# The rows of the second norm turned by VectorE and DRAM instead of TensorE, in a transformer block of Strassen products

## The chip, the cores and the metric

One core of one Trainium2 chip. The time is device microseconds of the program on that core, the median of the runs that are named beside it. The profile is that of one execution; its own time is given beside its span.

## The reference

What is computed is one transformer block with conditioning, in float32: 8 sequences of 1024 tokens, width 512, 16 heads of 32, hidden width 2048, all with biases.

```python
mod = silu(condition) @ Wada + bada
sh_a, sc_a, gt_a, sh_m, sc_m, gt_m = split(mod, 6)
xm = layernorm(x, g1, be1) * (1 + sc_a) + sh_a
x = x + gt_a * attention(xm, Wqkv, Wproj, bproj)      # causal, 16 heads
xm = layernorm(x, g2, be2) * (1 + sc_m) + sh_m
x = x + gt_m * (gelu(xm @ W1 + b1) @ W2 + b2)
```

## The kernel before

**Blocks and windows.** The tokens are cut into 16 blocks n of 512, two per sequence; an even n is the first half of a sequence, an odd n the second. All products of rows and weights (q, k, v, the projection, up, down) are of Strassen's kind with seven products of half size instead of eight; a step named T1 to T4 is a sum of quarters of the rows, S1 to S4 one of the weights. The quarters of the rows are B11, B21, B22 and T1 in the tile `xm` (features on partitions, tokens in the row) and T2, T3, T4 in the tile `t`. One product takes two weight pieces (128x512, 256 KB), and each piece is used by 16 matmuls of 32 columns x 256. The seven products of one step go through three PSUM banks; each is evicted by VectorE (L197, a sum with an earlier partial result such as u2 or u4) or ScalarE (L192, a copy), and the next product that needs this bank waits for that.

**The order of the work** is written by a planner in Python, while the program is built. It keeps a modelled clock for each engine (`now`), and the instructions of each engine come in the order in which the planner issues them. Attention of block n (scores L1602, their maxima on VectorE L1619, the second scores L1683 and L1695, the exponential on ScalarE L1708, the weighted sum L1736) is spread over the linear steps of window n, which the table `plan` lists. In window w the block n = w - 1 is projected, normed and taken through up and down, and q, k of block w + 1 and v of block w are made. `fetch` (L336) loads weight pieces nine ahead on SP's queue, each when a piece nine earlier has been used.

**From rows to `xm`.** `normalize` (L617) makes statistics on VectorE and the normed rows on ScalarE (L653). `modulated` (L732) turns them, so that features come to the partitions, and applies the gain and the shift that the conditioning gives. It does so in two ways, and `is_turned` (L377) chooses:

- by TensorE: for each of four chunks of features, four 128x128 transposes into a PSUM bank (L769), then gain and shift on the way out of the bank, by ScalarE (L784) or VectorE (L778). Before the change all blocks of the second norm go this way, and blocks 0 to 3 of the first.
- by VectorE and DRAM (`turn_rows`, L702): four transposes of 32x32 squares on VectorE (L708), four DMAs that put the squares of 32 partitions into a DRAM tile (`put`, L719), one DMA that gets the whole tile back in the turned order (`get`, L725), then gain and shift in place in SBUF (L784, L778). Before the change blocks 4 to 15 of the first norm go this way. The DMAs are kept in the list `transfers` and issued on SP's queue by `run_transfers` (L575), one after the other as the modelled clock passes; the apply is planned for 5000 ns after the get.

Both are followed by T1 (L792) and T2, T3, T4 (L794, and L162 or L165 by VectorE or GpSimd).

**The residual** rows (`xr`) of a block are loaded by four DMAs in `load_xr`, get the projection and the down products added on VectorE and GpSimd (L162, L165), and are stored by `store` (L1189) in four DMAs, two after each half. Those are on SP's queue too, in which every DMA waits for its own inputs, with all that stand behind it.

Of the kernel before, what the change touches and what calls it, by code (L numbers as in the profile page):

```python
# [22 lines left out]
def kernel(  # L23
# [176 lines left out]

    def matmul(ps, lhsT, rhs, start, stop, reads=(), bank=None):

        for j in range(HPG):
            r = slice(j * hd, (j + 1) * hd)
            nc.tensor.matmul(  # L205
                ps[r, :], lhsT[:, r], rhs, start=start, stop=stop, skip_group_check=True
            )
# [30 lines left out]
        0: [("load_xa", 2), ("preps",), ("k", 1), ("norm_a", 2), ("gates", "a"), ("q", 1)]  # L238
        + [("mod", 4), ("at", 2), ("v", 1), ("mod", 3), ("gates", "m")],
    }  # L240
    late = []
    for w in range(1, NB):
        n = w - 1
        m = mlp_steps(n)
        even = blocks[n][1] == 0
        rows_a = [("rows", blocks[n][0], "a")] if even else []
        rows_m = [("rows", blocks[n][0], "m")] if even else []
        own = m[:1] + ([("load_xa", w + 2)] if w + 2 < NB else []) + m[1:3]
        own += [("norm_a", w + 2)] if w + 2 < NB else []
        if w == NB - 1:  # L250
            steps = late[:1] + [("load_xr", n)] + rows_a + [("proj", n), ("mt", n)] + late[1:]
            steps += [("v", w)] + rows_m + own + m[3:6]
            late = m[6:]
        else:

            steps = late + [("v", w), ("load_xr", n)] + rows_a + [("proj", n), ("k", w + 1)]
            if w == 1:
                steps = [("load_xr", n)] + rows_a + [("k", w + 1), ("proj", n)]
            steps += [("mt", n), ("q", w + 1)] + rows_m + own
            at = [("at", w + 2)] if w + 2 < NB else []  # L260
            if blocks[w][1] == 0:

                late = m[3:4] + at + m[4:]
            else:
                steps += m[3:4] + at + m[4:6]
                late = m[6:]
        plan[w] = steps
    n = NB - 1
    plan[NB] = [("load_xr", n), late[0], ("beside", ("proj", n)), late[1], ("mt", n)] + mlp_steps(n)

    plain_proj = (NB - 2, NB - 1)
    kept_sums = {}
# [99 lines left out]
    cond_sb = tmp.tile([P, TB], F32, tag="y", name="cond_sb")[:B, :]  # L372
    nc.sync.dma_start(cond_sb, cond)

    SQ = 32
# [326 lines left out]
    def turn_rows(key, tiles, xm):  # L702

        squares = xm.rearrange("p c (j r) -> p (c j) r", r=P)
        there = kept.tile([D, TB], F32, tag=f"turned_{int(key[1:]) % 2}", name=f"turned_{key}")

        def turn(t):
            nc.vector.transpose(  # L708
                squares[:, :, ts(t, SQ)], tiles[t].rearrange("p (k r) -> p k r", r=SQ)
            )  # L710
            note("DVE", 700, [("hat", key, t)], [])
            if t == NTT - 1:
                ready = now["DVE"] + SYNC
                for a in range(P // SQ):
                    transfers.append((ready, lambda a=a: put(a)))
                transfers.append((ready + 5000, get))

        def put(a):
            nc.sync.dma_start(  # L719
                there[:, ts(a, P)].rearrange("(k r) n -> r k n", r=SQ),  # L720
                squares[a * SQ : (a + 1) * SQ, :, :],
            )

        def get():
            nc.sync.dma_start(xm, there.rearrange("(c p) n -> p c n", p=P))  # L725
            written["spread", key] = queue_free[0] + 5000

        written["spread", key] = NEVER
        for t in range(NTT):
            add_job(lambda t=t: turn(t), [("hat", key, t)])  # L730

    def modulated(key, gain, shift, b, guards):  # L732
        for t in ("B11", "B21", "B22", "T1", "T2", "T3", "T4"):
# [77 lines left out]
        return bank  # L811

    qTs, kTs, vs = {}, {}, {}
    projected, valued = set(), set()
    xm_of, hTs, hidden = {}, {}, set()

    SUMS = (("S1", "A21", "A22", ALU.add), ("S2", "S1", "A11", ALU.subtract),
# [78 lines left out]
    def strassen(step, x, dest, target, row, done, put=None, after={}):  # L896
# [14 lines left out]
        def product(a, t, bank=None):  # L911
            start = bank is None
            reads = [(x, t)] + ([("sums", *step, a)] if raw and a[0] == "S" else [])
            for i in range(2):
                for k in range(2):
                    if i + k:
                        yield [], []
                    elif start:
                        yield reads, [BANK]
                        bank = lin_bank()  # L920
                    else:
                        yield reads, [("l", bank)]
# [3 lines left out]
                    lhsT, rhs = (second, first) if row else (first, second)  # L926
                    matmul(
                        banks[bank][:, ts(i, HB)], lhsT[:, ts(i, P)], rhs,
                        start and i + k == 0, k == 1, reads, bank,
                    )  # L930
# [57 lines left out]
        tail_key[0] = key  # L988
        start(tail())

    def project_T(step, store, pool, tag, done):

        n = step[1]
        dst = pool.tile([P, NC, TB], F32, tag=tag, name=f"{tag}_{n}")
# [100 lines left out]
    def project_out(n):  # L1095
# [7 lines left out]
        last = n == NB - 1  # L1103
        begun = []

        def begin(t):

            bank = yield from accumulate(
                [(attT[:, c, ts(t, P)], piece(at[c])) for c in range(NC - 1)], [("att", n)], False
            )  # L1110
            begun.append(bank)

        for t, xt in enumerate(tiles):
            if last:
                while len(begun) <= max(t, 1):
# [1 line left out]
                bank = begun[t]  # L1117
                yield [("att", n, t)], []
                matmul(
                    banks[bank], attT[:, NC - 1, ts(t, P)], piece(at[NC - 1]), False, True,  # L1120
                    [("att", n, t)], bank,
                )
            else:
                bank = yield from accumulate(
                    [(attT[:, c, ts(t, P)], piece(at[c])) for c in range(NC)], [("att", n)]
                )
            y = tmp.tile([P, D], F32, tag="y", name=f"y_{n}_{t}", bufs=2)
            ky = y_key("proj", True)
# [59 lines left out]

    def store(n, t):  # L1189
        b, h = blocks[n]  # L1190
        for i in (2 * t, 2 * t + 1):
            r0 = h * TB + i * P
            nc.sync.dma_start(out[b, r0 : r0 + P, :], residual[n][:, i, :])
        stored[n + 1] = max(stored.get(n + 1, 0.0), due([("xr", n, 2 * t), ("xr", n, 2 * t + 1)]))

    def down(n, part):
# [19 lines left out]
        def product(operand):  # L1216
# [3 lines left out]
            for i in range(NQ):  # L1220
                p = next(at)
                for k in range(2):
                    c = 2 * i + k
                    hT = hTs[n, 2 * kh + c // NC][:, c % NC, tokens]
                    for m in range(2):
# [3 lines left out]
                        else:  # L1229
                            yield [], []  # L1230
                        matmul(
                            banks[bank][:, ts(m, HB)], hT[:, ts(m, P)], halves(p)[:, k, :],
                            c + m == 0, c == 2 * NQ - 1, reads, bank,
                        )
                release(p)
# [94 lines left out]
    def perform(step):  # L1330
# [12 lines left out]
        elif kind == "load_xr":  # L1343
            n = step[1]
            b, h = blocks[n]
            if n == NB - 2:
                xr = kvp.tile([P, NTT, D], F32, tag="kT", name=f"xr_{n}")
            else:
                xr = xrp.tile([P, NTT, D], F32, tag="xr", name=f"xr_{n}")
            residual[n] = xr  # L1350
            for t in range(NTT):
                r0 = h * TB + t * P
                nc.sync.dma_start(xr[:, t, :], x[b, r0 : r0 + P, :])
                landed = max(now["PE"], stored.get(n, 0.0)) + LANDING + 700 * t
                written["xr", n, t] = landed
        elif kind == "norm_a":
            key = f"a{step[1]}"
# [466 lines left out]
    def attend():  # L1824
        previous = None
        for n in range(NB):
# [19 lines left out]
            stream["rate"] = planned_time(n) / mine * (0.7 if n == 0 else 1.0)  # L1846
            written["free for k", n + 2 if n % 2 else n + 1] = 0.0
            written["free for k", n + 1] = 0.0
            for g, k, n_slots, upto in slots:
                if (n, g) == groups[-1]:  # L1850
                    margin[0] = -2000
# [66 lines left out]
    needs = sum(exp_need(parts) for n in range(NB) for g in range(NC) for parts in weight_units(n, g))  # L1918
    needs += sum(score_need(*unit) for unit in units)
    for n in range(NB):  # L1920
        written["attended", n] = NEVER
        written["v done", n] = NEVER
        written["m used", n] = NEVER
# [79 lines left out]
```

## Time and profile before

| | before |
| --- | --- |
| median of 3 runs | 3483.92 us (3483.72 to 3483.95) |
| the profiled execution, its own time | 3487.44 us |
| its span, from the first to the last instruction | 3485.7 us |
| granted TensorE clock | 1.000 |
| TensorE busy in the span | 3448.3 us |

In the page's groups, a row reads: line, engine, operation, output <- inputs by the program's names (numbers left out), shapes, count | busy us, mean ns of one | idle of the engine just before them, and what ended it. A row of the waits reads: engine, tile, line <- what was waited for: us in total, times, longest. A row of a timeline reads: start in us from the span's start, duration, engine, line, operation, tiles, count, and in brackets the idle before it with its releaser. A row of the DMAs reads: tiles, queue, kind, count, size of one, median us from issue to landing. One float32 matmul leaves two records in the trace. PE is TensorE, DVE VectorE, ACT ScalarE, POOL GpSimd, SP SyncE with its DMA queue.

### The profile page before, as it was taken

The page shows a single profiled execution, that of the slowest core. Times are in us where ns is not written, and L with a number is a line of the kernel's source. Part 1 is how long each engine was busy: PE and PEld are TensorE (multiplying, and loading weights), DVE is VectorE, ACT ScalarE, POOL GpSimd, SP SyncE. Part 2 cuts the span into 40 slices and gives each one's busy share as a digit, 9 for nine tenths or more (in the row PEclk, how much of TensorE's full clock was granted, in tenths as well). Part 3 has the DMA queues.
Part 4 walks back from the last instruction along what each step waited for, and adds up shares of the span by engine and source line. Part 5 has one row for each costly group of instructions (what it writes and reads, how often), then busy time and mean ns, then how long its engine had stood idle before and what let it go on. Part 6 is the DMA issues. An engine that isn't in the chain of part 4 may idle for free.

```text
span 3485.7 us, 122756 instructions
## 1 busy us (share of the span) xinstructions
PE 3448.3 (99%) x55618; PEld 1776.1 (51%) x55618; DVE 1905.0 (55%) x2136; ACT 1286.7 (37%) x1420; POOL 2074.5 (60%) x2209
## 2 busy tenths in 40 slices
PE   8999999999999999999999999999999999999999
PEld 5544455445554554545545455454554545545445
DVE  6765664554645556465564655645546455554463
ACT  2335243352433524235152352514524244241531
POOL 3676755675466664576645766557664576644640
PEclk9999999999999999999999999999999999999999
DMA  6843334335353353633536335363443534435334
GB/s 213 271 144 86 117 110 150 120 105 172 107 167 102 105 174 104 186 95 100 173 98 186 98 111 159 101 186 98 129 140 101 183 101 135 130 100 153 90 121 136
DMA packets 350523, 466.84 MB, mean 134 GB/s; under 512 B 27460, under 2 KB 212092, under 8 KB 350004
## 3 DMA queue, kind: packets, MB, share of 16 engines
q1 hardware_dynamic: 349808, 458.73, 43.8%
q8 instruction: 438, 7.18, 0.9%
q14 instruction: 81, 0.66, 0.1%
q10 hardware_dynamic: 196, 0.28, 0.0%
HBM read 416.90 MB, written 41.99 MB: 132 GB/s over the span
## 4 chain that ended last, share of the span: by engine, by line
PE 94%; DVE 3%; POOL 1%; ACT 1%; issue 0%; DMA 0%; SPq 0%; DVEq 0%; ACTq 0%; POOLq 0%
PE bank L205 65%; PE sc L1602 9%; PE po L1736 8%; PE st L1695 7%; PE st L1683 3%; DVE mx L1619 2%; PE bank L1757 2%; PE bank L769 1%; PE bank L1657 1%; POOL pT L1821 0%; DVE sc L1616 0%; POOL mcols L1640 0%; DVE pT L1818 0%; POOL mcols L1641 0%; DMA ada<-in_L_cond_Wada_dram 0%
## 5 line engine op out<-in xcount | busy, mean ns | idle before, releaser
L1821 POOL TENSOR_TENSOR pT<-pT,pT 128x256 f32<-128x256 f32 (+3 forms) x1254 | 1174.5, 972 | 210.3 <-ACT pT L1708 119.2
L1708 ACT ACTIVATE pT<-st 128x2048 f32<-128x2048 f32 x288 | 541.1, 1879 | 1001.1 <-PE st L1695 908.8
L205 PE MATMUL bank<-w,hT 128*32 128x256 f32 x14336 | 795.5, 379 | 0.0
L1619 DVE TENSOR_REDUCE mx<-sc 128x4 f32<-128x2048 f32 (+3 forms) x384 | 665.6, 1754 | 140.3 <-PE sc L1602 133.7
L205 PEld LDWEIGHTS bank<-w,hT 128*32 128x32 f32 x14336 | 448.8, 110 | 335.6 <-issue 29.2
L205 PE MATMUL bank<-xm_m,w 128*32 128x256 f32 x8192 | 498.8, 380 | 0.0
L205 PE MATMUL bank<-t_m,w 128*32 128x256 f32 x6144 | 384.2, 380 | 0.1
L205 PEld LDWEIGHTS bank<-xm_m,w 128*32 128x32 f32 x8192 | 253.6, 110 | 238.8 <-issue 76.0
L1713 POOL TENSOR_SCALAR_AFFINE_SELECT pT<-pT 128x512 f32<-128x512 f32 x256 | 164.8, 661 | 308.8 <-ACT pT L1708 306.9
L1602 PE MATMUL sc<-kT,qT 32*128 32x512 f32 (+3 forms) x3072 | 329.1, 520 | 2.9 <-DVE mx L1619 1.9
L1616 DVE TENSOR_TENSOR sc<-sc,mask 128x1024 f32<-128x1024 f32 (+1 forms) x160 | 162.9, 1018 | 276.2 <-PE sc L1602 217.6
L1736 PE MATMUL po<-pT,v 128*32 128x512 f32 (+3 forms) x3072 | 306.0, 493 | 0.0
L1695 PE MATMUL st<-qT,kT 32*128 32x512 f32 (+3 forms) x3072 | 299.8, 486 | 0.0
L205 PEld LDWEIGHTS bank<-t_m,w 128*32 128x32 f32 x6144 | 193.0, 110 | 180.8 <-issue 54.2
L205 PE MATMUL bank<-xm_a,w 128*32 128x256 f32 x3968 | 248.8, 381 | 1.3 <-ACT xm_a L784 1.1
L197 DVE TENSOR_TENSOR hT<-bank,u_u 128x512 f32<-128x512 f32 x192 | 129.1, 686 | 151.2 <-PE bank L205 149.0
L165 POOL TENSOR_TENSOR qT<-top,rec 128x512 f32<-128x512 f32 x60 | 77.1, 1285 | 219.8 <-ACT rec L1775 219.8
L1602 PEld LDWEIGHTS sc<-kT,qT 32*128 32x128 f32 x3072 | 129.4, 183 | 150.9 <-ACT pT L1708 61.8
L205 PE MATMUL bank<-w,qT 128*32 128x256 f32 (+1 forms) x2944 | 191.4, 399 | 1.3 <-DVE qT L1782 1.3
L1153 ACT ACTIVATE hT<-hT,cols 128x512 f32<-128x512 f32 x256 | 164.2, 711 | 55.0 <-DVE hT L197 54.4
L205 PE MATMUL bank<-t_a,w 128*32 128x256 f32 x2944 | 183.3, 380 | 0.0
L165 POOL TENSOR_TENSOR hT<-hT,hT 128x1024 f32<-128x1024 f32 x28 | 79.7, 2868 | 167.6 <-DVE hT L1211 167.6
(232 smaller groups left out, 3507.5 us busy)
## 6 DMA issues: line engine op xcount, KB each, us to landing
w<-in_L_cond_W_dram SPq DMA_DIRECT2D x384, 256.0 KB, 2.9
w<-kept_up_S SPq DMA_DIRECT2D x256, 256.0 KB, 2.6
w<-kept_down_S SPq DMA_DIRECT2D x256, 256.0 KB, 2.8
w<-kept_qkv_S SPq DMA_DIRECT2D x180, 256.0 KB, 2.7
w<-in_L_cond_Wqkv_dram SPq DMA_DIRECT2D x147, 256.0 KB, 3.0
hat<-in_x_dram SPq DMA_DIRECT2D x64, 256.0 KB, 4.7
xr<-in_x_dram SPq DMA_DIRECT2D x64, 256.0 KB, 4.6
out_dram<-xr SPq DMA_DIRECT2D x64, 256.0 KB, 2.6
```

The costliest lines, as they stand in the source:

```text
L165: nc.gpsimd.tensor_tensor(out, a, b, op)
L197: nc.vector.tensor_tensor(out, src, other, op)
L205: nc.tensor.matmul(ps[r, :], lhsT[:, r], rhs, start=start, stop=stop, skip_group_check=True)
L1153: nc.scalar.activation(hT[:, i, :], hT[:, i, :], AF.Gelu, bias=cols[:, O_B1 + f : O_B1 + f + 1])
L1602: nc.tensor.matmul(sc[:, j, c0 : c0 + w], qTs[n][r, gg, ts(qt, P)], keys_of(n, kh)[r, gg, :w], start=True, stop=True, skip_group_check=True,)
L1616: nc.vector.tensor_tensor(place, place, shape_of.to_broadcast(place.shape), ALU.add)
L1619: nc.vector.tensor_reduce(maxima[n, gg][:, kh, qt, :], sc[:, :, c0 : c0 + w], axis=AX.X, op=ALU.max)
L1695: nc.tensor.matmul(st[:, j, c0 : c0 + w], kT[r, gg, ts(k % NTT, P)], qT[r, gg, TB - w :], start=False, stop=True, skip_group_check=True,)
L1708: nc.scalar.activation(pT[:, :, :used], st[:, :, :used], AF.Exp, scale=scale)
L1713: nc.gpsimd.affine_select(diagonal, diagonal, pattern=[[0, HPG], [1, P]], compare_op=ALU.is_ge, fill=0.0, base=0, channel_multiplier=-1,)
L1736: nc.tensor.matmul(po[r, TB - w :], v[:, k % NTT, g * P + j * hd : g * P + (j + 1) * hd], pT[:, j, c0 : c0 + w], start=(k == 0), stop=last ...
L1821: nc.gpsimd.tensor_tensor(into, into, pT[:, j, c0 : c0 + w], ALU.add)
```

## The change

The second norm's rows of blocks 4 to 14 take the second way too (`is_turned`). In the squares that VectorE turns, tokens come out in a permuted order unless the rows come in permuted; for these blocks the residual's rows are therefore loaded and stored in the permuted order (`row_tiles_of`), and the projection and the down products take their stationary columns by `token_tile`. The quarters B11, B21, B22 and T1 of such a block are then two (feature chunks) x four runs of 64 tokens with a step of 128, so that up's moving operand has three dimensions (`matmul`).

The residual of odd blocks lives in a spare key buffer (`key_tag`), with a wait of the planner for the buffer ("free for xr") and for the keys (`keyed`). `run_transfers` takes the transfer that is ready first and no longer the first in the list. The order of steps in a window becomes: the residual's load, v, projection, the second norm (`mt`), the older down parts, q, k, then up; before it was the late up and down parts, v, residual's load, projection, k, `mt`, q, up. Lines of the kernel after are some 20 to 40 higher: L205 becomes L208, L769 becomes L794.

```diff
     def matmul(ps, lhsT, rhs, start, stop, reads=(), bank=None):
+        if len(rhs.shape) == 3:
+            ps = ps.rearrange("p (a n) -> p a n", a=rhs.shape[1])
         for j in range(HPG):
             r = slice(j * hd, (j + 1) * hd)
+            columns = lhsT[:, j, :] if len(lhsT.shape) == 3 else lhsT[:, r]
             nc.tensor.matmul(
-                ps[r, :], lhsT[:, r], rhs, start=start, stop=stop, skip_group_check=True
+                ps[r], columns, rhs, start=start, stop=stop, skip_group_check=True
             )
...
+    SQ = 32
+    def token_tile(columns, i, n):
+        if is_turned(f"m{n}"):
+            return columns.rearrange("p (a t r) -> p t a r", t=2, r=SQ)[:, i]
+        return columns[:, ts(i, P)]
+    def row_tiles_of(rows, n):
+        if is_turned(f"m{n}"):
+            tiles = rows.rearrange("(h a t r) d -> h t a r d", h=2, t=2, r=SQ)
+            return [tiles[i // 2, i % 2] for i in range(NTT)]
+        return [rows[ts(i, P), :] for i in range(NTT)]
...
-    late = []
+    late, downs = [], []
...
-            steps = late + [("v", w), ("load_xr", n)] + rows_a + [("proj", n), ("k", w + 1)]
...
-            steps += [("mt", n), ("q", w + 1)] + rows_m + own
...
+        head = rows_a + [("load_xr", n)]
...
+        elif w < NB - 1:
+            steps = late + head + [("v", w), ("proj", n), ("mt", n)] + downs + [("q", w + 1), ("k", w + 1)]
+        else:
+            steps = late + head + [("v", w), ("proj", n), ("mt", n)] + downs
+        cut = m[2] if blocks[w][1] == 0 else None
+        i = ups.index(cut) if cut in ups else len(ups)
+        plan[w] = steps + rows_m + ups[:i]
+        late, downs = ups[i:], m[4:]
...
     def is_turned(key):
-        return key[0] == "a" and int(key[1:]) >= 4
+        n = int(key[1:])
+        return n >= 4 if key[0] == "a" else 4 <= n < NB - 1
...
     def run_transfers(everything=False):
-        while transfers and (
-            everything or max(queue_free[0], transfers[0][0]) <= now["PE"]
-        ):
-            ready, transfer = transfers.pop(0)
+        while transfers:
+            i = min(range(len(transfers)), key=lambda i: transfers[i][0])
+            if not everything and max(queue_free[0], transfers[i][0]) > now["PE"]:
+                return
+            ready, transfer = transfers.pop(i)
             queue_free[0] = max(queue_free[0], now["PE"], ready) + 700
             transfer()
...
+        if rows_turned and key[0] == "m":
+            tokens = xm.rearrange("p c (a h n) -> p c h a n", h=2, n=2 * SQ)
+            part["B11"], part["T1"] = tokens[:, one, 0], tokens[:, one, 1]
+            part["B21"], part["B22"] = tokens[:, two, 0], tokens[:, two, 1]
+            for i, t in enumerate(("T2", "T3", "T4")):
+                part[t] = sums[:, i, :, :].rearrange("p c (a n) -> p c a n", n=2 * SQ)
...
+    def key_tag(n):
+        return "odd_kT" if n % 2 else f"even_kT_{n // 2 % 2}"
...
     def store(n, t):
         b, h = blocks[n]
+        rows = row_tiles_of(out[b, h * TB : (h + 1) * TB, :], n)
         for i in (2 * t, 2 * t + 1):
-            r0 = h * TB + i * P
-            nc.sync.dma_start(out[b, r0 : r0 + P, :], residual[n][:, i, :])
+            nc.sync.dma_start(rows[i], residual[n][:, i, :])
...
-            if n == NB - 2:
-                xr = kvp.tile([P, NTT, D], F32, tag="kT", name=f"xr_{n}")
+            if n % 2:
+                yield [("free for xr", n)], []
+                spare = key_tag(min(n + 3, NB))
+                xr = kvp.tile([P, NTT, D], F32, tag=spare, name=f"xr_{n}", bufs=1)
             else:
                 xr = xrp.tile([P, NTT, D], F32, tag="xr", name=f"xr_{n}")
...
-            for t in range(NTT):
-                r0 = h * TB + t * P
-                nc.sync.dma_start(xr[:, t, :], x[b, r0 : r0 + P, :])
+            for t, rows in enumerate(row_tiles_of(x[b, h * TB : (h + 1) * TB, :], n)):
+                nc.sync.dma_start(xr[:, t, :], rows)
...
-            yield from project_T(step, kTs, kvp, "kT", lambda: None)
+            yield from project_T(step, kTs, kvp, "kT", lambda: keyed.add(step[1]))
...
     def next_scores():
-        until(lambda: units[unit_at[0]][0] in projected)
+        until(lambda: units[unit_at[0]][0] in projected & keyed)
```

More of the change, by code (lines that the diff above doesn't have):

```diff
@@ L704, in turn_rows @@
         squares = xm.rearrange("p c (j r) -> p (c j) r", r=P)
-        there = kept.tile([D, TB], F32, tag=f"turned_{int(key[1:]) % 2}", name=f"turned_{key}")
+        there = kept.tile([D, TB], F32, tag=f"turned_{key[0]}{int(key[1:]) % 2}", name=f"turned_{key}")
         def turn(t):
@@ L925, in product @@
                     first, second = w[a][:, k, :], xm_of[x][t][:, k, :]
-                    lhsT, rhs = (second, first) if row else (first, second)
+                    if x[0] == "p":
+                        lhsT, rhs = token_tile(second, i, int(x[1:])), first
+                    else:
+                        lhsT, rhs = (second, first) if row else (first, second)
+                        lhsT = lhsT[:, ts(i, P)]
                     matmul(
-                        banks[bank][:, ts(i, HB)], lhsT[:, ts(i, P)], rhs,
+                        banks[bank][:, ts(i, HB)], lhsT, rhs,
                         start and i + k == 0, k == 1, reads, bank,
@@ L989, in strassen @@
         start(tail())
+    def key_tag(n):
+        return "odd_kT" if n % 2 else f"even_kT_{n // 2 % 2}"
     def project_T(step, store, pool, tag, done):
         n = step[1]
-        dst = pool.tile([P, NC, TB], F32, tag=tag, name=f"{tag}_{n}")
+        if tag == "kT":
+            dst = pool.tile([P, NC, TB], F32, tag=key_tag(n), name=f"{tag}_{n}", bufs=1)
+        else:
+            dst = pool.tile([P, NC, TB], F32, tag=tag, name=f"{tag}_{n}")
         store[n] = dst
@@ L1104, in project_out, with tokens @@
         begun = []
+        def tokens(c, t):
+            return token_tile(attT[:, c, half(t // 2, HB)], t % 2, n)
         def begin(t):
             bank = yield from accumulate(
-                [(attT[:, c, ts(t, P)], piece(at[c])) for c in range(NC - 1)], [("att", n)], False
+                [(tokens(c, t), piece(at[c])) for c in range(NC - 1)], [("att", n)], False
             )
@@ L1119, in project_out @@
                 matmul(
-                    banks[bank], attT[:, NC - 1, ts(t, P)], piece(at[NC - 1]), False, True,
+                    banks[bank], tokens(NC - 1, t), piece(at[NC - 1]), False, True,
                     [("att", n, t)], bank,
@@ L1124, in project_out @@
                 bank = yield from accumulate(
-                    [(attT[:, c, ts(t, P)], piece(at[c])) for c in range(NC)], [("att", n)]
+                    [(tokens(c, t), piece(at[c])) for c in range(NC)], [("att", n)]
                 )
@@ L1848, in attend @@
             written["free for k", n + 1] = 0.0
+            written["free for xr", n - 1] = 0.0
             for g, k, n_slots, upto in slots:
@@ L1920 @@
     for n in range(NB):
+        written["free for xr", n] = 0.0 if n == NB - 1 else NEVER
         written["attended", n] = NEVER
```

35 lines of the change are left out of this document (15 added, 20 removed).

## The prediction

> **What bounds the kernel now.** I read the page first (span, busy shares, the chain that ended last), then TensorE's groups and waits, then timelines of single stretches.
>
> ```profile
> span 3485.7 us, 122756 instructions
> PE 3448.3 (99%) x55618; PEld 1776.1 (51%) x55618; DVE 1905.0 (55%) x2136; ACT 1286.7 (37%) x1420; POOL 2074.5 (60%) x2209
> PE 94%; DVE 3%; POOL 1%; ACT 1%; issue 0%; DMA 0%; SPq 0%; DVEq 0%; ACTq 0%; POOLq 0%
> ```
>
> TensorE is busy 99% of the span and is 94% of the chain, so two things count: PE time taken away is gained, and any new PE wait is lost in full. What the change wants to take away is this group and its waits (groups and waits of PE):
>
> ```profile
> L769 PE MATMUL bank<-ident,xh_m 128*128 128x128 f32 x256 | 41.2, 286 | 3.0 <-ACT xm_m L784 2.2 <-ACT xh_m L653 0.7
> PE bank L769 <- ACT xm_m L784: 2.2, 7, 0.4
> PE bank L205 <- ACT xm_a L784: 1.1, 1, 1.1
> ```
>
> Means overlap in a pipelined PE, so the price is read from start to start in one block's 16 transposes (timeline, PE: start, duration, line):
>
> ```profile
> 897.09 0.66 PE L769 MATMUL bank<-ident,xh_m 128*128 128x128 f32 x4
> 897.68 0.40 PE L1683 MATMUL st<-mrow,minus_ones 32*128 32x256 bf16 x8
> 897.91 1.03 PE L1695 MATMUL st<-qT,kT 32*128 32x256 f32 x16
> 898.87 1.07 PE L1736 MATMUL po<-pT,v 128*32 128x384 f32 x16
> 899.87 1.31 PE L769 MATMUL bank<-ident,xh_m 128*128 128x128 f32 x10
> 901.11 1.14 PE L1602 MATMUL sc<-kT,qT 32*128 32x512 f32 x8
> 902.18 0.44 PE L769 MATMUL bank<-ident,xh_m 128*128 128x128 f32 x2
> 902.55 0.64 PE L205 MATMUL bank<-xm_m,w 128*32 128x256 f32 x8
> ```
>
> 0.59 + 1.24 + 0.37 = 2.20 us for 16, changes of tile shape included. The same rows price attention pieces: a score set st 1.19 (897.68 to 898.87), a po 1.00, an sc 1.07. A weight piece of a linear product (16 matmuls, 32 records) takes 1.73:
>
> ```profile
> 1034.05 1.90 PE L205 MATMUL bank<-w,xm_a 128*32 128x256 f32 x32
> 1035.78 1.90 PE L205 MATMUL bank<-w,t_a 128*32 128x256 f32 x32
> ```
>
> **What is removed.** Blocks 4 to 14 lose their transposes: 11 x 2.20 = 24.2 us of PE, and 11/16 of the 3.0 us of idle before L769, 2.1. Together 26.3 us, if nothing else became late.
>
> **What is added, off PE.** Per block four 32x32 stream transposes on DVE, four stores into DRAM and one load back on SP's queue, then gain and shift in SBUF, then T1, T2, T4. The path exists for the first norm (12 blocks), so its prices are there:
>
> ```profile
> L708 DVE STREAM_TRANSPOSE xm_a<-hat 128x512 f32<-128x512 f32 x48 | 30.8, 683 | 0.0
> L778 DVE TENSOR_SCALAR xm_m<-bank,gainm,shiftm 128x512 f32<-128x512 f32 x16 | 12.9, 809 | 22.9 <-PE bank L769 22.4
> L792 DVE TENSOR_TENSOR xm_m<-xm_m 128x512 f32<-128x512 f32 x16 | 11.9, 741 | 1.0
> L794 DVE TENSOR_TENSOR t_m<-xm_m 128x512 f32<-128x512 f32 x16 | 14.4, 902 | 3.9 <-ACT xm_m L784 3.6
> L197 DVE TENSOR_TENSOR qT<-bank,u_q 128x512 f32<-128x512 f32 x48 | 32.9, 688 | 40.2 <-PE bank L205 39.6
> turned_a<-xm_a SPq DMA_DIRECT2D x48, 256.0 KB, 4.2
> xm_a<-turned_a SPq DMA_DIRECT2D x12, 1024.0 KB, 5.6
> ```
>
> 44 x 0.683 = 30 us more on a DVE that is 55% busy costs nothing as work; the cover is DVE's idle 45%, and it is gone only where DVE stands still behind a wait. That is the point of the case: the applies and T1, T2, T4 stand in DVE's and ACT's queues **ahead of PSUM evictions that PE needs**, and they wait for the load. How long after the last store is the apply possible? Two of the turns of the first norm (SP's and ACT's timelines):
>
> ```profile
> 1000.16 0.82 SPq L719 DMA_DIRECT2D turned_a<-xm_a  x1
> 1004.49 0.37 SPq L725 DMA_DIRECT2D xm_a<-turned_a  x1
> 1010.15 2.94 ACT L784 ACTIVATE xm_a<-xm_a,shifta,gaina 128x512 f32<-128x512 f32 x4 [9.79 <-DMA xm_a<-turned_a]
> ```
> ```profile
> 1227.77 0.43 SPq L719 DMA_DIRECT2D turned_a<-xm_a  x1
> 1233.27 0.37 SPq L725 DMA_DIRECT2D xm_a<-turned_a  x1
> 1238.86 2.94 ACT L784 ACTIVATE xm_a<-xm_a,shifta,gaina 128x512 f32<-128x512 f32 x4 [13.49 <-DMA xm_a<-turned_a]
> ```
>
> 10.0 and 11.1 us from the last store's issue; ACT idled 9.8 and 13.5 us before it, which was free there because nothing behind it was due. [...]
>
> The stores themselves can be late. SP works in order, and an output store waits for POOL's residual adds:
>
> ```profile
> 1028.17 1.28 POOL L165 TENSOR_TENSOR p_d<-p_d,u_d 128x512 f32<-128x512 f32 x1 [0.97 <-DVE u_d L197]
> 1030.89 1.28 POOL L165 TENSOR_TENSOR xr<-xr,p_d 128x512 f32<-128x512 f32 x1
> 1032.19 2.02 SPq L1193 DMA_DIRECT2D out_dram<-xr  x2
> ...
> 1035.07 1.28 POOL L165 TENSOR_TENSOR y_d<-y_d,row_gm 128x512 f32<-128x512 f32 x1 [2.91 <-DVE y_d L197]
> 1037.74 0.83 SPq L1193 DMA_DIRECT2D out_dram<-xr  x2
> ```
>
> From the end of a down product, the u3 kind frees SP after 0.69 (eviction) + 4.0 + 0.8 to 2.0 = 5.5 to 6.7 us; the y21 kind after 0.69 + 2.7 + 0.8 = 4.2.
>
> **Where the new waits fall**, from the order of the changed kernel's instructions on each engine:
>
> - Blocks 5 and 7. The u3 output stores stand between the first and the second turn store. Time 0 is the end of the u3 product: three turn stores and two weight fetches behind it (0.4 each, about 1.8 to the last one's issue) put the last store at 7.3 to 8.5, the apply at 17.3 to 19.6. DVE's order is two applies, T1, one apply, T2, T4 (0.81 x 3 + 0.74 + 0.90 x 2 = 5.0), then the eviction of q's fourth sum (0.69), which frees the bank that q's product wants: 23.0 to 25.3. PE has ten pieces until then, 17.3. **Wait 5.7 to 8.0 each.**
> - Blocks 9, 11, 13. The y21 output stores stand ahead of the last turn store: issue at 4.2 after that product's end, apply at 14.2 to 15.3, two applies on ACT (1.6), T1, one apply, T2, T4 on DVE (4.2 less what the third apply overlaps, say 3.5), q's eviction 0.69: 20.0 to 21.1. PE has eight pieces, 13.8. **Wait 6.2 to 7.3 each.**
> - Block 14. The first up product follows at once. u3's stores free SP at 5.5 to 6.7, then four turn stores and three fetches, last at 7.6 to 8.6; load at 17.6 to 19.7, two applies, 19.2 to 21.3. PE has four pieces (6.9) and about seven attention pieces of 1.0 to 1.2 (7.4), 14.3. **Wait 4.9 to 7.0.**
> - Blocks 4, 6, 8, 10, 12: the applies stand amid attention on ACT. Taken at 0.3 each (2.2 over 7 in the row of L769's waits); up to 1.1 by the xm_a row. The first norm's turns of even blocks now also fall amid attention: taken 0.5 each for five, between 0 and the 2.9 of a run of four applies. Together 4, between 0 and 20.
>
> Sum of waits: 2 x 6.9 + 3 x 6.8 + 6.0 = 40, plus 4: **44 us, from 33 to 64**. Against 26.3 saved: **+18 us** (from +7 to +38).
>
> **Costed at nothing.** The permuted residual rows are still whole rows of 2 KB in as many DMAs of 256 KB; odd blocks' residual in a spare key buffer makes its load earlier, not later. The up products of the 11 blocks read a moving operand in four chunks of 64 instead of 256 in a row (2816 matmuls, 5632 records). No row has that. Nearest are groups with different operands, whose means (third row: the first norm's) lie within 2 ns:
>
> ```profile
> L205 PE MATMUL bank<-w,hT 128*32 128x256 f32 x14336 | 795.5, 379 | 0.0
> L205 PE MATMUL bank<-xm_m,w 128*32 128x256 f32 x8192 | 498.8, 380 | 0.0
> L205 PE MATMUL bank<-xm_a,w 128*32 128x256 f32 x3968 | 248.8, 381 | 1.3 <-ACT xm_a L784 1.1 <-DVE xm_a L778 0.2
> ```
>
> I take 0 and keep 2 ns x 5632 = 11 us either way. [...]
>
> The new order of steps (downs ahead of q and k) moves weight fetches with the products; nine pieces are held ahead, 9 x 1.73 = 15.6 us, longer than SP's longest hold above.
>
> **The rivals.**
> 1. *Hidden, faster.* The waits vanish if the applies come before DVE's queue is needed. For blocks 5 and 7 the chain of 5.7 us must start by 17.3 - 5.7 = 11.6, that is 3 to 4 us after the last store, or the stores must go out 6 us earlier. For it: PE's waits are tiny now although twelve turns run. Against: 10.0 and 11.1 measured, and those twelve had no eviction behind them. Time: 3484 - 26 = 3458; with a third of the waits left, 3472.
> 2. *Half hidden, no change.* POOL or the second output store comes sooner than its row, or the load lands 3 us sooner: six waits shorter by 3 us each, -18, net 0: 3484. [...]
> 3. *More late.* The strided operand at its bound of 11 us, or the even blocks at theirs (16 more): 3513 to 3518.
> 4. *It doesn't do what it says*: 176 of 256 of these transposes are gone from PE's order, so no chance is left for it.
>
> **How the numbers follow.** The sum stands against the profiled execution (span 3485.7, its own time 3487.4, 3.5 above the median of the runs shown): 3487.4 + 18 = 3505; against the median of 3483.9 it is 3502. I name 3502. A measurement here tells about 0.2%, 7 us, from no change. Chances: the forecast 0.52, more late 0.09 (both slower by over 0.2%: 0.61), half hidden 0.18, hidden 0.21. The range leaves out the fully hidden end and the far late end: 3465 (all but 7 us of the waits hidden, -19) to 3519 (+35). The forecast's own range is 3491 to 3514.
>
> **What the profile after would show.** PE's L794 group (now L769) at x80; a 5 to 8 us idle of PE on a DVE eviction (qT, u_q) in each of blocks 5 to 13's odd stretches, ended by the load of the turned rows behind it; output stores ahead of turn stores on SP; about 6 us before block 14's first up product. Wrong would be: PE's waits in all under 50 us, an apply within 5 us of the last store, or up products with a mean above 382 ns.

## The result and the profile after

The kernel after takes 3586.6 us (3583.4 to 3588.7, 4 runs) against 3483.8 for the kernel before: ratio 1.0295, 95% interval 1.0277 to 1.0313. The forecast was 3502, in a range from 3465 to 3519. The sign held, and most of the added time is waits of the kind that was forecast; the size was more than five times too small, and 22 us of it come from a step that was costed at nothing, the new order.

The page of the kernel after, its parts 1 and 4:

```profile
span 3581.7 us, 122448 instructions
PE 3443.3 (96%) x55442; PEld 1774.9 (50%) x55442; DVE 2045.9 (57%) x2240; ACT 1285.1 (36%) x1425; POOL 2041.8 (57%) x2140
PE 84%; DVE 5%; DMA 5%; ACT 2%; POOL 1%; issue 1%; SPq 1%; DVEq 0%; ACTq 0%; POOLq 0%
```

PE has 176 instructions less and is busy 5 us less, but it now stands idle for 138.4 us of its span (3581.7 - 3443.3) where it stood for 37.4 before. The list of PE's waits, kernel after:

```profile
PE bank L208 <- DVE qT L197: 32.6, 2, 16.6
PE bank L1696 <- POOL mcols L1680: 18.8, 12, 2.1
PE bank L208 <- DMA w<-kept_up_S: 16.3, 1, 16.3
PE st L1722 <- DVE mx L1658: 13.0, 16, 2.4
PE bank L208 <- DVE u_q L197: 11.2, 2, 5.7
PE bank L208 <- DMA w<-in_L_cond_Wqkv_dram: 9.5, 2, 4.9
PE bank L208 <- ACT xm_m L809: 9.1, 1, 9.1
```

Evictions (qT, u_q) and applies stand where they were forecast. New are waits on weight pieces, and two waits inside attention (mcols, mx) have grown, from 7.3 and 2.4 us before. One block, 9, shows it all (kernel after, timeline of SP, then ACT, DVE and PE):

```profile
2192.51 1.23 SPq L1231 DMA_DIRECT2D out_dram<-xr  x2
2194.40 1.02 SPq L738 DMA_DIRECT2D turned_m<-xm_m  x1
2203.62 1.66 SPq L1231 DMA_DIRECT2D out_dram<-xr  x2
2205.33 0.65 SPq L738 DMA_DIRECT2D turned_m<-xm_m  x1
2214.25 0.36 SPq L744 DMA_DIRECT2D xm_m<-turned_m  x1
```
```profile
2219.51 2.22 ACT L809 ACTIVATE xm_m<-xm_m,shiftm,gainm 128x512 f32<-128x512 f32 x3 [20.62 <-DMA xm_m<-turned_m]
```
```profile
2193.12 0.69 DVE L197 TENSOR_TENSOR y_d<-bank,u_d 128x512 f32<-128x512 f32 x1 [3.52 <-PE bank L208]
2221.06 0.69 DVE L817 TENSOR_TENSOR xm_m<-xm_m 128x512 f32<-128x512 f32 x1 [18.61 <-ACT xm_m L809]
2223.65 1.28 DVE L197 TENSOR_TENSOR qT<-bank,u_q 128x512 f32<-128x512 f32 x2
```
```profile
2224.39 3.64 PE L208 MATMUL bank<-t_a,w 128*32 128x256 f32 x32 [16.28 <-DMA w<-kept_up_S]
2227.80 3.73 PE L208 MATMUL bank<-xm_a,w 128*32 128x256 f32 x64
```

DVE stands 18.6 us ahead of T1; the eviction of qT comes behind it at 2223.65, and PE goes on at 2224.39. The list puts this wait down to a weight piece of up, which q's product does not read; what fits is the eviction, whose first half ends 0.69 us after its start, at 2224.3; in blocks 11 and 13 the same wait is put down to qT. The rows also show the piece after the wait: 3.41 us from start to start instead of 1.73.

The clock says why (kernel after, windows: length, busy of PE, PEld, DVE, ACT, POOL with counts, PEclk, DMA share, GB/s):

```profile
2215.00:2220.00 5.00, 0.00 (x0) 0.00 (x0) 0.00 (x0) 0.49 (x1) 0.00 (x0) 0.50 0.88 312
2220.00:2225.00 5.00, 0.61 (x8) 0.39 (x12) 3.74 (x6) 2.20 (x4) 1.77 (x1) 0.50 0.76 267
2225.00:2230.00 5.00, 5.00 (x72) 2.47 (x66) 0.69 (x1) 0.12 (x1) 0.00 (x0) 0.70 0.18 48
2230.00:2235.00 5.00, 5.00 (x100) 2.76 (x92) 1.38 (x2) 0.47 (x1) 0.00 (x0) 1.00 0.51 145
```

The granted clock is 0.50 in the wait and stays there for 3.6 us of work behind it: the 0.70 of the window from 2225 is 3.0 us at 0.50, so up to 2228.0, and PE goes on at 2224.39. So I split each run's span in three: idle (span less PE busy), clock (over windows of 2.5 us, PE busy times one less the granted clock), and work (the rest of PE busy).

| profiled execution | span | idle | clock | work |
| --- | --- | --- | --- | --- |
| before | 3485.7 | 37.4 | 1.6 | 3446.7 |
| after | 3581.7 | 138.4 | 19.2 | 3424.1 |
| no turn, new order | 3508.5 | 52.2 | 8.1 | 3448.2 |
| no turn, old order | 3482.9 | 35.9 | 0.0 | 3447.1 |
| output stores on GpSimd | 3549.5 | 112.0 | 14.3 | 3423.2 |
| apply late | 3567.3 | 121.0 | 17.3 | 3429.0 |
| both | 3535.4 | 87.5 | 22.4 | 3425.5 |
| both, load on GpSimd | 3552.7 | 106.4 | 18.7 | 3427.6 |
| five output stores left out | 3510.0 | 76.8 | 10.1 | 3423.1 |
| five output stores later, 14 on TensorE | 3500.2 | 66.2 | 8.3 | 3425.7 |
| the same, apply 3 us later in 9, 11, 13 | 3495.4 | 60.6 | 9.5 | 3425.3 |
| even blocks alone | 3514.0 | 66.3 | 7.9 | 3439.8 |
| even blocks alone, stores later | 3500.7 | 52.1 | 11.3 | 3437.3 |
| turn, old order | 3626.8 | 148.4 | 40.3 | 3438.1 |

### The profile page after: what moved, and what is told of

It is laid out like the page before. It is cut to its first block, busy times and chain, and to the rows that moved or that the text cites. A ratio compares the mean times of both kernels' runs of the same rounds, so it can differ in the third digit from the quotient of the medians.

```text
span 3581.7 us, 122448 instructions
## 1 busy us (share of the span) xinstructions
PE 3443.3 (96%) x55442; PEld 1774.9 (50%) x55442; DVE 2045.9 (57%) x2240; ACT 1285.1 (36%) x1425; POOL 2041.8 (57%) x2140
## 4 chain that ended last, share of the span: by engine, by line
PE 84%; DVE 5%; DMA 5%; ACT 2%; POOL 1%; issue 1%; SPq 1%; DVEq 0%; ACTq 0%; POOLq 0%
PE bank L208 58%; PE sc L1641 8%; PE po L1775 7%; PE st L1734 6%; PE st L1722 2%; DVE mx L1658 2%; PE bank L1796 2%; DMA w<-kept_proj_S 1%; DMA turned_m<-xm_m 1%; DVE sc L1655 1%; ACT pT L1747 1%; DMA xr<-in_x_dram 1%; DMA xm_m<-turned_m 1%; DVE hT L1249 1%; POOL pT L1860 1%
## 5 line engine op out<-in xcount | busy, mean ns | idle before, releaser
L1860 POOL TENSOR_TENSOR pT<-pT,pT 128x256 f32<-128x256 f32 (+3 forms) x1254 | 1234.4, 1020 | 165.0 <-ACT pT L1747 127.2
L208 PE MATMUL bank<-w,hT 128*32 128x256 f32 x14336 | 816.5, 380 | 1.7 <-ACT rec L1806 1.6
L208 PEld LDWEIGHTS bank<-w,hT 128*32 128x32 f32 x14336 | 453.8, 110 | 367.5 <-issue 83.1
L208 PE MATMUL bank<-xm_m,w 128*32 128x256 f32 x8192 | 501.2, 381 | 9.1 <-ACT xm_m L809 9.1
L208 PE MATMUL bank<-t_m,w 128*32 128x256 f32 x6144 | 384.2, 380 | 0.1
L208 PEld LDWEIGHTS bank<-xm_m,w 128*32 128x32 f32 x8192 | 256.0, 110 | 233.0 <-issue 60.2
L208 PEld LDWEIGHTS bank<-t_m,w 128*32 128x32 f32 x6144 | 190.4, 110 | 179.7 <-issue 55.8
L208 PE MATMUL bank<-xm_a,w 128*32 128x256 f32 x3968 | 248.4, 389 | 25.1 <-DVE u_q L197 11.2
L208 PE MATMUL bank<-t_a,w 128*32 128x256 f32 x2944 | 186.0, 389 | 48.8 <-DVE qT L197 32.6
L208 PE MATMUL bank<-w,qT 128*32 128x256 f32 (+1 forms) x2944 | 193.5, 400 | 0.0
L208 PEld LDWEIGHTS bank<-xm_a,w 128*32 128x32 f32 x3968 | 128.6, 112 | 128.3 <-issue 33.2
```

The source lines that it names most:

```text
L208: nc.tensor.matmul(ps[r], columns, rhs, start=start, stop=stop, skip_group_check=True)
L1860: nc.gpsimd.tensor_tensor(into, into, pT[:, j, c0 : c0 + w], ALU.add)
```

## The experiments

Theory Q: PE waits for evictions that stand in VectorE's or ScalarE's queue behind the apply of rows that come back late. Rivals: the new order of steps itself (O); the turn's DMAs are slow whatever stands ahead (D); weight pieces held on SP, not evictions (S).

**1. The order alone.** In `is_turned`:

```diff
-        return n >= 4 if key[0] == "a" else 4 <= n < NB - 1
+        return key[0] == "a" and n >= 4
```

> The kernel after with no row of the second norm turned by VectorE (all 16 blocks keep TensorE's transposes); the new order of steps, the first-ready transfer and the residual in key buffers stay. Theory Q (PE's waits are evictions that stand behind the applies of rows that come back late from DRAM, and the clock that falls after each): the six long waits and the clock loss go, the 176 transposes come back: 3484 to 3506 us, no PE wait over 3 us beside the start. Rival O (the new order of steps itself leaves PE short): 3540 us or more, with waits of 5 us and more at the same places.

Measured 3509.9 us, ratio to before 1.0063 (1.0048 to 1.0078), just over Q's range, far under O's. The long waits are gone, so the turn makes them. But the order costs 22 us by itself. The list of PE's waits, and the place of one of them in the timelines of DVE and PE, in the run of the order alone:

```profile
PE bank L1696 <- POOL mcols L1680: 14.1, 9, 2.1
PE st L1722 <- DVE mx L1658: 10.4, 14, 1.7
```
```profile
1056.40 3.49 DVE L1249 TENSOR_TENSOR hT<-hT,hT 128x1024 f32<-128x1024 f32 x2
1059.82 2.29 DVE L162 TENSOR_TENSOR hT<-hT,hT 128x1024 f32<-128x1024 f32 x1
1062.03 1.22 DVE L1655 TENSOR_TENSOR sc<-sc,mask 128x1024 f32<-128x1024 f32 x1
1065.56 1.30 DVE L1672 TENSOR_TENSOR mx<-mx 128x16 f32<-128x16 f32 x1
```
```profile
1069.50 0.62 PE L1696 MATMUL bank<-ident_b,mcols 128*32 128x128 bf16 x16 [2.08 <-POOL mcols L1680]
```

With the down parts where they now stand, their sums (hT, 5.8 us) come on DVE ahead of the mask and the maxima of a score, and attention's next step waits. Idle is 14.8 us more than before (mcols 14.1 instead of 7.3, mx 10.4 instead of 2.4), clock 6.5.

**2. The old order without the turn.** Experiment 1, and the table `plan` of the kernel before.

> The kernel after with no row of the second norm turned by VectorE and the old order of steps: what is left of the change is the residual of odd blocks in key buffers and the first-ready transfer. If the new order of steps is what cost 22 us in the run of the order alone: within 7 us of before, 3478 to 3492 us. If the buffers or the waits for the keys cost it: 3500 us or more.

Measured 3485.2 us, ratio 1.0000 (0.9991 to 1.0010). The key buffers, the first-ready transfer and the waits for the keys cost nothing; the 22 us are the order of steps.

**3. The turn in the old order.** The kernel after with the `plan` of before.

> The kernel after with the order of steps of before (k after the projection, only q between the second norm and up). If the new order was needed to cover the turn: the planner has 14 pieces of q and then attention alone between norm and up, PE waits 5 to 15 us in each of the 11 blocks, 3560 to 3660 us. If the order alone costs 22 us and the turn could have been covered by attention: 3500 to 3560 us.

Measured 3633.4 us (2 runs), ratio 1.0426 (1.0405 to 1.0447). With only q between norm and up, attention's scores wait for their own maxima; that attention has been used up there as cover is argued, not shown. PE's waits in this run, first row:

```profile
PE st L1721 <- DVE mx L1657: 48.0, 25, 6.6
```

So the new order is dear, and the turn without it is dearer.

**4. Output stores on GpSimd's queue.**

```diff
-            nc.sync.dma_start(rows[i], residual[n][:, i, :])
+            nc.gpsimd.dma_start(rows[i], residual[n][:, i, :])
```

> The kernel after with the output stores issued by GpSimd, behind its residual adds, and no longer by SP. Theory Q with SP's hold behind the output stores as the cause of the lateness: blocks 9, 11, 13 wait 3 to 7 us instead of 17, blocks 5 and 7 1 to 5 instead of 10, the last turn store goes out within 3 us of the y21 product's end instead of 12: 3515 to 3550 us. Rival D (the turn's store and load take 14 us by themselves in this place, whatever stands ahead): waits within 3 us of now, 3570 us or more. Rival O: 3580 to 3590 us.

Measured 3558.7 us, ratio 1.0213 (1.0196 to 1.0230), between the two. SP's hold is gone: in block 9 the last turn store goes out 0.7 us after the eviction of y21 begins, as Q had it. The weight waits of blocks 5 and 7 are gone too; their eviction waits are 5.8 and 5.6. Blocks 9, 11 and 13 wait 10.9, 13.0 and 9.6 instead of 16.3, 15.9 and 16.6. SP's timeline of this run in block 9 shows what is left:

```profile
2171.39 0.32 SPq L738 DMA_DIRECT2D turned_m<-xm_m  x1
...
2175.55 1.18 SPq L738 DMA_DIRECT2D turned_m<-xm_m  x1
2176.82 4.61 SPq L367 DMA_DIRECT2D w<-kept_qkv_S  x1
2188.81 0.36 SPq L744 DMA_DIRECT2D xm_m<-turned_m  x1
```

Four stores are out in 4.2 us, and the load still goes out 13.3 us after the last one, because that wait is for the stores to land. In the first norm's turns of the kernel before it was 3.9 to 5.7, and the last store had landed 3.8 to 5.6 after its issue.

**5. Five blocks' output stores left out** (the output rows of blocks 4, 6, 8, 10 and 12 are not written).

```diff
+        if n in (4, 6, 8, 10, 12):
+            return
```

> The kernel after without the output stores of blocks 4, 6, 8, 10 and 12, whose rows are left out of the output: neither the hold on SP nor their DMA traffic stands beside the turns of 5, 7, 9, 11 and 13. Against the run with the stores on GpSimd it differs by the traffic alone. If the traffic of the output stores is what makes the turn stores land late: last turn store to load 4 to 6 us instead of 13, waits of 9, 11, 13 at 2 to 6 us, 3510 to 3530 us. If not: waits of 9 to 13 us there as with the stores on GpSimd, 3545 to 3560 us.

Measured 3513.5 us, ratio 1.0079 (1.0064 to 1.0094). SP's timeline in block 9:

```profile
2166.17 1.17 SPq L738 DMA_DIRECT2D turned_m<-xm_m  x1
...
2172.19 0.36 SPq L744 DMA_DIRECT2D xm_m<-turned_m  x1
```

Last store to load 6.0, 4.1 and 6.0 us in blocks 9, 11, 13; their waits are 3.0, 2.2 and 4.6, those of 5 and 7 at most 1.5. Beside these turns, what differs from experiment 4, where it was 13.3 in block 9, is the traffic of the output stores. So these stores harm the turn twice: by their hold on SP, and by their DMA beside the turn's. Rival D is right only beside them. Experiment 9 shows what is special about them: the order of their rows.

**6. The apply planned later.**

```diff
-            written["spread", key] = queue_free[0] + 5000
+            written["spread", key] = queue_free[0] + (14000 if key[0] == "m" else 5000)
```

> The kernel after with the apply of the second norm's turned rows planned for 14000 ns after the load's issue instead of 5000, so that it stands some five pieces (9 us) later in VectorE's and ScalarE's queues. Theory Q: what counts is what stands behind the apply; each long wait falls by about 9 us, the six to 20 to 35 us in all instead of 84, the clock loss to under 12: 3505 to 3545 us. Rival S (SP's late weight fetches hold PE, not the evictions): the waits stay within 3 us of now and are ended by weight pieces, 3570 us or more. Rival O: 3580 to 3590 us.

Measured 3571.5 us, ratio 1.0242 (1.0226 to 1.0257). The time is S's, the waits are Q's and S's: those of 9, 11 and 13 fell from 17 to 8 us and that of 14 from 9.1 to 1.9, but 5 and 7 still wait 10.3 and 11.7, and all of these but that of 14 end on weight pieces. PE's waits, first row, and one of them in PE's timeline:

```profile
PE bank L208 <- DMA w<-kept_qkv_S: 45.6, 10, 10.1
```
```profile
2211.58 3.64 PE L208 MATMUL bank<-t_a,w 128*32 128x256 f32 x32 [6.55 <-DMA w<-kept_qkv_S]
```

With the evictions out of the way, the weight pieces are next: they stand on SP behind the output stores and behind the load's wait for its stores (in block 9 the load goes out at 2210.84, 9.1 us after the last turn store).

**7. Both edits, 4 and 6.**

> Output stores issued by GpSimd and the apply planned for 14000 ns after the load's issue. The run with the late apply alone moved PE's wait from the evictions to weight pieces, which stood on SP behind the output stores and behind the load's wait for the turn stores. Theory Q (all of it is queueing): without the output stores on SP the weight pieces are late only by the load's own wait; long waits 10 to 35 us in all, 3505 to 3535 us. Rival D (the turn's DMAs land in 13 us instead of 4 to 5 there, and SP's wait at the load holds the weights): weight waits of 5 us and more stay in blocks 9, 11, 13, 3535 to 3560 us.

Measured 3537.9 us, ratio 1.0152 (1.0135 to 1.0169). Long waits in the turned places are 2.3 to 3.6 us now. But the clock lost 22.4 us, and another queue shows the same pattern, ScalarE's, in the first norm's turn of an even block (ACT, then PE):

```profile
2310.67 2.93 ACT L809 ACTIVATE xm_a<-xm_a,shifta,gaina 128x512 f32<-128x512 f32 x4 [8.20 <-DMA xm_a<-turned_a]
2313.51 1.85 ACT L1747 ACTIVATE pT<-st 128x2048 f32<-128x2048 f32 x1
```
```profile
2315.41 1.14 PE L1641 MATMUL sc<-kT,qT 32*128 32x512 f32 x8 [4.02 <-ACT pT L1747]
```

An exponential stands behind an apply that waits 8.2 us for its rows, and PE waits 4.0 for the exponential.

**8. The load on GpSimd's queue too.** As 7, with the `get` of second-norm rows issued by GpSimd.

> As the run with both edits, and the load of the second norm's turned rows is issued by GpSimd too, so that its wait for the turn stores holds no weight piece on SP. Theory Q: nothing that PE needs stands behind the turn's waits any more in blocks 5 to 13; long waits under 15 us in all, clock loss under 9: 3490 to 3512 us, that is the run of the order alone (3508 span) less up to 24 us of transposes plus what is left. If waits move to GpSimd's sums of the weights of attention or its residual adds instead: 3515 us or more.

Measured 3556.1 us, ratio 1.0204 (1.0189 to 1.0219): a miss for Q, in the range that was given for waits that move to GpSimd's work. Many of the waits went into attention (PE's waits, first and third row):

```profile
PE st L1723 <- DVE mx L1659: 21.3, 19, 3.1
...
PE sc L1642 <- ACT pT L1748: 15.1, 5, 7.2
```

GpSimd sums the parts of the weights of attention, and in block 10 it is idle for 4.9 us just ahead of the load. That each of these waits comes from it is argued, not shown.

**9. Even blocks alone** (4, 6, 8, 10, 12).

> The kernel after with only blocks 4, 6, 8, 10 and 12 turned by VectorE (odd blocks and 14 by TensorE). Theory Q: the even blocks' applies stand amid attention and cost next to nothing; 5 x 2.2 us of PE less than with the order alone, no wait over 3 us: 5 to 12 us below the run of the order alone, 3475 to 3500 us. Rival E (turning costs the same wherever it stands, by DMA traffic): 5/11 of the loss, 3530 us.

Measured 3516.3 us, ratio 1.0084 (1.0069 to 1.0099): a miss. Work fell by 8.4 us, but weight pieces were late in the *odd* blocks' linear stretches, 18.6 us in all, where no row of the second norm is turned (PE):

```profile
2193.55 3.02 PE L208 MATMUL bank<-t_a,w 128*32 128x256 f32 x29 [2.43 <-DMA w<-kept_qkv_S]
```

The run of the order alone has no such wait, though SP issues the same DMAs in the same order in this stretch. What differs in this stretch is the row order of the even block's output stores: permuted here, one row after the other there. By the trace's record of landings, the 20 permuted stores of this run land 6.2 to 12.1 us after their issue, the 42 others of `store` 2.0 to 4.6; the ten weight pieces issued between and behind the stores of block 8 land after 8.7 to 10.8 us, in the order alone after 2.8 to 5.1. Eight microseconds from the first of these stores, in the order alone and then here (windows):

```profile
2179.20:2187.20 8.00, 8.00 (x153) 4.81 (x148) 1.72 (x3) 1.18 (x2) 2.55 (x2) 1.00 0.90 298
2175.20:2183.20 8.00, 8.00 (x152) 4.81 (x148) 1.72 (x3) 1.17 (x2) 2.55 (x2) 1.00 0.53 163
```

The DMA engines are busy 0.53 of the time instead of 0.90, and move 163 GB/s instead of 298, while the pieces are late. So the permuted rows make the stores slow, and all that stands behind them on SP with them. A permuted store's rows are four runs of 32, and its landing has 5 signals in the record of the kernel after, where a plain store's has 16. Of the 16 signals of the first weight piece behind the u3 stores of block 9 there, 12 come within 3.3 us of its issue and four after 7.3 to 8.7. Why a permuted store is slow, no run here shows.

**10. Even blocks alone, their output stores 30 us later.** The change to `store`, also used in 11 and 12:

```diff
-        for i in (2 * t, 2 * t + 1):
-            nc.sync.dma_start(rows[i], residual[n][:, i, :])
+        xr = residual[n]
+        def send():
+            for i in (2 * t, 2 * t + 1):
+                nc.sync.dma_start(rows[i], xr[:, i, :])
+        if n in (4, 6, 8, 10, 12):
+            transfers.append((now["PE"] + 30000, send))
+        else:
+            send()
```

> Only blocks 4, 6, 8, 10 and 12 turned by VectorE, and the output stores of these blocks 30000 ns later. The run with the even blocks alone had weight pieces late behind the output stores on SP (18.6 us). Theory Q: these go, and 11 us of transposes come off the run of the order alone: 3490 to 3502 us. If an even block's turn costs by itself: 3508 us or more.

Measured 3495.3 us, ratio 1.0025 (1.0015 to 1.0034). The weight waits went, and the even turn itself is free, with its stores moved to a place where nothing waits for them: work is 10.9 us under the order alone, idle is the same (52.1 against 52.2).

**11. All odd and even blocks but 14, the stores later.**

> The kernel after with the output stores of blocks 4, 6, 8, 10 and 12 planned 30000 ns later, past the turn of the next block, and block 14 left to TensorE. Theory Q with both halves (the stores' hold on SP and their traffic): as in the run that left these stores out, but complete, and without block 14's wait of 8 us and its clock loss: 3495 to 3512 us; waits of 2 to 5 us in blocks 9, 11, 13, none over 2 in 5 and 7. If the stores only move their harm to the place where they now stand: 3520 us or more.

Measured 3505.3 us, ratio 1.0056 (1.0041 to 1.0071). Waits in 9, 11, 13 are 2.9, 1.7, 2.6; blocks 5 and 7 keep 2.6 and 2.5, a little more than expected.

**12. The same, with the apply of 9, 11 and 13 planned 3 us later.**

> The same, with the apply of blocks 9, 11 and 13 planned 3000 ns later, one eviction further back in VectorE's queue. Theory Q: their remaining waits of 2 to 5 us shrink to under 2 without weight pieces becoming late: 4 to 12 us below the run without this edit. If the weight pieces behind the load's wait are next: no gain, and waits that end on a weight piece.

Measured 3493.4 us, ratio 1.0024 (1.0014 to 1.0035), 12 us less; of these the profiled executions show 4.8. The waits of 9, 11 and 13 are under 1 us, and no weight piece is late there; block 7 waits 3.5. This is the best version with the turn, 93 us under the kernel after and still 8 above before. What is left are mostly the waits that the order makes (14.1 and 10.4 us in experiment 1; PE's waits, first two rows of this run):

```profile
PE bank L1704 <- POOL mcols L1688: 18.8, 12, 2.1
PE st L1730 <- DVE mx L1666: 10.5, 14, 1.4
```

No version tried beats the kernel before.

## Why the prediction was wrong

**What is removed: right.** Forecast 24.2 us of PE work. The kernel after against the order alone, which differ by the turn only: 3448.2 - 3424.1 = 24.1.

**The strided operand at nothing: right.** The up products' group has a mean of 381 ns after, 380 before, and the work agrees to 0.1 us.

**Where the new waits fall: right in place, wrong in size.** PE waits in the six blocks named: 10.6 and 10.2 us in 5 and 7 (two waits each), 17.3, 16.9 and 17.7 in 9, 11 and 13 (with a first wait of 1.0), 9.1 in 14. Sum 82 against a forecast of 40. Three steps failed:

- *"Blocks 9, 11, 13. The y21 output stores stand ahead of the last turn store: issue at 4.2 after that product's end."* In block 9 that product's eviction begins at 2193.12; the last turn store went out at 2205.33, 12.2 later. I had started SP's clock fresh at y21, but u3's output stores had already held SP until 2192.51, and the seven DMAs that had piled up came out one behind the other, 1.4 us each, where the forecast has 0.4 for one in blocks 5 and 7 and none here. Then the stores landed late: 8.9 us to the load instead of 4.3 to 5.5, beside the output stores' traffic. The apply came 26.4 us behind the product instead of 14.2 to 15.3.
- *"Nine pieces are held ahead, longer than SP's longest hold above."* One hold is shorter, but u3's stores, the turn's issues and the load's wait for its stores add up. In block 5 (PE's timeline of the kernel after) the first of two waits is a weight piece, not forecast; the second is the eviction, 5.7 us, at the lower end of the forecast of 5.7 to 8.0:

```profile
1319.75 3.41 PE L208 MATMUL bank<-xm_a,w 128*32 128x256 f32 x32 [4.87 <-DMA w<-in_L_cond_Wqkv_dram]
1328.83 3.64 PE L208 MATMUL bank<-xm_a,w 128*32 128x256 f32 x32 [5.68 <-DVE u_q L197]
```

- *"The permuted residual rows are still whole rows of 2 KB in as many DMAs of 256 KB."* Rows and bytes are the same, but not the time. By the landings in the trace of the kernel after, the 44 permuted output stores land after 6.0 to 11.2 us (median 8.2), the 18 others of `store` after 2.0 to 4.4 (3.0); the permuted loads of the residual after a median of 11.3 instead of 4.2. In block 9 the two u3 stores land after 6.3 and 8.8 us, and the first weight piece behind them after 8.7. This was costed at nothing. The slow stores stand ahead of the late DMAs in both steps above; how much of the 82 us they make was not measured, since no run keeps the turn and stores its rows in another form.

**"The new order of steps moves weight fetches with the products": wrong.** Costed at nothing, it is 22 us (experiments 1 and 2). I had asked of the order only what SP holds, and not what DVE has ahead of attention's maxima.

**The even blocks at 0.3 each: right** (experiment 10), once the output stores are out of the way.

**A term was missing: the clock.** 17.6 us of the 96 us of span are work at a lower clock behind the waits.

The sum, between the profiled executions of before and after: work -22.6 (-24.1 by the turn, +1.5 by the order), idle +101.0 (14.8 by the order, 86.2 by the turn and its stores), clock +17.6 (6.5 and 11.1): +96.0. Forecast was +18 from 44 of waits. The rival *more late* had the right sign, but neither of its two causes came true; the rivals *hidden* and *half hidden* fell. What stays open: why a permuted store is slow, how much of the 82 us would go with it, and why the clock lost more in experiment 7 than in others with longer waits.

## What to carry to other kernels

When a saved operation becomes a round trip, list for every in-order queue on its way, the DMA-issuing one too, all that stands ahead of it back to the queue's last free moment, and add those holds up; a queue that was held one step earlier doesn't start fresh. Price a DMA whose rows change their order as a new DMA, even when the bytes and the length of a row stay: here a store landed after a median of 8.2 us instead of 3.0 and a load after 11.3 instead of 4.2, and a weight piece behind two such stores after 8.7. Price a move of steps by the order in which each engine then sees its work, attention's small reductions included. In this kernel, whose TensorE was 99% busy, the waits cost their length, 101.0 us more than before, and slower stretches behind them, 17.6 us.

## What the runs showed of the hardware

Behind some PE waits of 2.1 us the granted clock was 0.50. In the run of the order alone, the PE wait of 2.08 us that ends at 1069.5 is followed by these windows:

```profile
1067.50:1070.00 2.50, 0.50 (x20) 0.50 (x24) 2.37 (x4) 1.88 (x1) 2.27 (x5) 0.89 0.28 93
1070.00:1072.50 2.50, 2.50 (x27) 0.68 (x20) 2.47 (x2) 0.59 (x1) 2.50 (x2) 0.50 0.02 7
1072.50:1075.00 2.50, 2.50 (x36) 0.92 (x32) 1.62 (x2) 0.00 (x0) 2.50 (x2) 0.93 0.00 0
```

The three windows lack (0.11 + 0.50 + 0.07) x 2.5 = 1.7 us of the clock, which is 3.4 us at 0.50, and PE is busy all through the last two. Not every such wait is followed by this: in the kernel after, PE waits 2.12 us for mcols until 1068.05, 1509.49 and 1951.21; behind the third the window from 1952.5 to 1955.0 is at 0.51, behind the first two the windows are at 1.00.

From the last turn store's issue to the load's it took 6.0, 4.1 and 6.0 us in blocks 9, 11 and 13 of experiment 5, beside weight loads, and 13.3 us in block 9 of experiment 4, where four output stores with permuted rows, 1 MB, went out in the same 6 us. In the kernel after, a plain output store of 256 KB lands 2.0 to 4.4 us after its issue, one with permuted rows 6.0 to 11.2; in experiment 9 it is 2.0 to 4.6 and 6.2 to 12.1, and on GpSimd's queue 2.4 to 4.6 and 6.7 to 13.5 (experiment 4).
